# Two 16-head attention stages: the matrix products of a turn sorted by their kind, and the steps of all other chains moved to even turns, two turns apart

## The chip, the cores and the metric

The kernel runs on one core of a Trainium2 chip. The metric is the device time of one execution in microseconds (us), the median of several runs. Besides the runs there is one profiled execution of the kernel, whose trace holds every instruction of every engine: TensorE (PE, with its weight loads as PEld), VectorE (DVE), ScalarE (ACT), GpSimd (POOL), and SyncE (SP), which issues the DMAs.

## The reference

The reference is a chain of eight layers on an input of 16 sequences of 256 tokens with 128 features: four times an attention or mixing layer followed by a feed-forward layer. Each is wrapped as `x = x + layernorm(f(layernorm(x)))`. Two of the layers hold a causal softmax attention with 16 heads of 8 features, and only these are touched by the change. The first ("L2 attention") in full:

```python
q = (x @ Wq).reshape(b, t, h, d) * scale      # h = 16, d = 8, scale = d ** -0.25
k = (x @ Wk).reshape(b, t, h, d) * scale
v = (x @ Wv).reshape(b, t, h, d)
dot = einsum('bqhd,bkhd->bhqk', q, k)
dot = where(causal, dot, -inf)
out = einsum('bhqk,bkhd->bqhd', softmax(dot), v).reshape(b, t, h * d)
return out @ Wo
```

The second ("L3 attention") is the second half of a larger layer. Its keys and values have 4 heads, each used by 4 query heads; q and k go through an RMS norm over the 8 features of a head and a rotary embedding before the products, and the output is projected and added to its own input.

## The kernel before, in words

**Data.** The tokens lie in SBUF as `NG = 8` groups of 512 tokens; a group is two sequences, and a sequence with its 16 heads is a batch here. So each attention stage has 16 batches. Each stage is a function that issues instructions for one group or batch at a time, written as Python generators: a `yield` ends a step, and `idle(n)` yields n times, that is, it leaves n - 1 steps empty.

**The planner.** `turns` (L392) sets the order by hand. An item is a generator with a starting turn. In each turn every item that has started takes one step, or up to three if it is behind; the instructions are issued in exactly that order. The items of a stage (L429) are the batches, newest first, then the heads of the groups 1 to 7 (which prepare a group), and last a chain of unrelated work named `beside`. Batch b of group g starts at turn 12g + 6b; its head starts `early` turns before 12g, 10 in the first stage and 26 in the second, where it is behind at turn 0 and catches up three steps a turn.

**A batch** (`attention`, L435) in turns counted from its start:

- 0, 2, 4 ("by query"): for each of four sets of four heads, the product of 32 rows of qT with km (each head's keys, zeroed but for its own 8 features), 32x128 weights against 512 columns, into four PSUM banks; behind each of the four a product of a 128x128 mask with the identity adds the causal mask; then DVE takes the negative maximum of each bank (L459, `at_nm`).
- 5: POOL splits the maxima into three bf16 pieces (L467, L469). 8: a pair of 128x128 products brings these pieces (`at_pc`) into the other layout, and ACT writes them as `at_mT` (L476).
- 11, 13, 15 ("by key"): four products of 32 rows of kT with qm, to which four bf16 products of ones with `at_mT` add the negative maxima; then ACT takes the exponential of each bank (L491, `at_e`), and POOL sets the masked entries to zero (L497, a selection).
- 16 to 21 ("values"): products of 128x32 weights `at_vm` with `at_e` into the one bank `o`.
- 22: ACT copies `o` to `at_oT` (L521). 23: four transposes of it. 25: DVE takes the reciprocal of the sums and scales (L530, L532, `at_y`). 26: two transposes of `at_y`, and ACT's copy `at_yT`.
- After the second batch of a group, its `tail` projects `at_yT` with `wo`, and adds the result to x.

Six turns later the next batch does the same, so that in the steady state an even turn issues one batch's query products and an older one's values, and an odd turn one batch's key products and an older one's values. Every 12 turns one head and one tail are added.

**PSUM.** `RING_BANKS` gives seven banks to the tag "s", which the tags "mm" and "t" share, and one bank to "o". So the four query banks, the four key banks and every projection or transpose take a bank out of the same seven, and wait until the engine that read it last (DVE for the maxima, ACT for the exponentials and most copies) has released it.

**The heads.** In the first stage (`stage_l2_attn`): norm of x (DVE L255, L257 and POOL L244, L245, then DVE L264), transposes to `xT`, products with wk and wq, `km` and `qm` (`variants`, two ACT and one POOL instruction each), and the product with wv, whose result ACT spreads into `at_vm` (L390). Its `beside` first ends two groups of the stage before (two DMAs named back), and then builds a table `lm` for the next stage: for each of 16 heads ACT L1402, three turns later POOL L1405, two turns later DVE L1407. In the second stage the head is `l3_rotated`: RMS norm, transposes, four products with `qkv`, ACT's copies of them into one buffer (L1598), POOL's squares (L1604), DVE's sums (L1609), ACT's square root (L1612, with a load of its table ahead of it), DVE's scaling of qkv in place (L1616), POOL's products with the cosines (L1622, L1623), DVE's with the sines (L1625, L1626) and the sums (L1628, L1629); then transposes of `rot` give kT and qT.

All products are issued in `mm` (L336), so their rows are told apart by their tiles.

Of the kernel before, what the change touches and what calls it, by code (L numbers as in the profile page):

```python
# [185 lines left out]
def idle(n):  # L186

    for _ in range(n):
        yield
# [10 lines left out]
class Ctx:  # L200
# [191 lines left out]
    def turns(self, items):  # L392


        now = 0
        items = [[start, 0, steps] for start, steps in items]
        while items:
            for item in items[:]:
                for _ in range(min(3, now - item[0] + 1 - item[1])):
                    item[1] += 1  # L400
                    if next(item[2], self) is self:
                        items.remove(item)
                        break
            now += 1

    def attention_stage(self, head, early, first, tail, beside=iter(())):

        got = [{} for _ in range(NG)]
        heads = [head(g, got[g]) for g in range(NG)]
        for _ in range(first):
            next(heads[0])
        self.attention_pools()  # L420
        for _ in heads[0]:
            pass

        def batch(g, b):
            yield from self.attention(g, b, got[g])
            if b == 1:
                yield from tail(g, got[g]["yT"])

        items = [(12 * g + 6 * b, batch(g, b)) for g in range(NG) for b in range(2)]  # L429
        items = items[::-1] + [(12 * g - early, heads[g]) for g in range(1, NG)] + [(9, beside)]  # L430
        with self.tc.manual_schedule():
            self.turns(items)

    def attention(self, g, b, got):
# [14 lines left out]
        for i in range(3):  # L449

            t, q, keys, vs = (0, q0, q0, slice(0, 4)) if i == 0 else (1, q1, both, slice(2 * i - 2, 2 * i))
            ss = [self.ps("s") for _ in rows]
            for k, s in zip(rows, ss, strict=True):
                self.mm(s, qT[k, q], km[k, vs, keys], True, False)
            for r, s in enumerate(ss):
                n = vs.stop - vs.start
                s = s.rearrange("p (v n) -> p v n", v=n)
                self.mm(s[:, :, t * P :], ident, bc(negmask, 1, n), False, True)
                v_.tensor_reduce(nm[:, t, r, vs], s, AX.X, ALU.max, negate=True)  # L459
            if i < 2:  # L460
                yield from idle(2)
        yield
# [14 lines left out]
        yield from idle(3)  # L477
# [3 lines left out]
        for i in range(3):  # L481
# [19 lines left out]
            if i < 2:  # L501
                yield from idle(2)
        yield

        o = self.ps("o")
        for v in range(4):
            reg = SEQ * (v // 2)
            for r, k in enumerate(rows):
                e = es[v // 2][:, r].rearrange("p (v n) -> p v n", v=2)[:, v % 2, :]
                self.mm(o[k, reg : reg + SEQ], vm[:, 2 * b, v, k], e, v == 0, False)  # L510
            yield
        for v in range(4):
# [4 lines left out]
            if v % 2:  # L517
                yield
# [3 lines left out]
        yield  # L522
# [3 lines left out]
        yield from idle(2)  # L526
# [6 lines left out]
        yield  # L533
# [746 lines left out]
def stage_l2_attn(k, x, w, xs, decays):  # L1280
# [9 lines left out]
    def head(g, got):  # L1290
        yield
        if g == 0:
            xn = k.t([P, NT, D], "xn", 1)
            k.normed_act(xn, x[g], *k.kept)
            yield from idle(3)
        else:
            xn = yield from k.norm(x[g], "xn", 1, 2)
            yield
# [9 lines left out]
        yield  # L1308
# [4 lines left out]
        yield  # L1313
# [261 lines left out]
def l3_rotated(k, xa, w, bufs=1, pool=None):  # L1575


    nc, v = k.nc, k.nc.vector
    sq = k.t([P, NT, D], "rms_sq", min(bufs, 2))
    nc.gpsimd.tensor_tensor(sq, xa, xa, ALU.mult)  # L1580
    yield from idle(3)
# [7 lines left out]
    yield  # L1589
# [5 lines left out]
    for t in range(NT):  # L1595
# [3 lines left out]
        if t % 2:  # L1599
            yield  # L1600
# [10 lines left out]
    yield  # L1611
    nc.scalar.activation(ss, ss, AF.Sqrt)  # L1612
    yield
# [10 lines left out]
    yield  # L1624
    v.tensor_tensor(tmp[:, :, :, 0:4], x2, trig["sin"], ALU.mult)  # L1625
    v.tensor_tensor(tmp[:, :, :, 4:8], x1, trig["sin"], ALU.mult)  # L1626
    yield from idle(2)
# [5 lines left out]
def l3_gqa(k, x, xa, w, gain, mix, first):  # L1633
# [5 lines left out]
    def head(g, got):  # L1639
# [5 lines left out]
        yield  # L1645
# [3 lines left out]
        yield  # L1649
        got["qT"] = k.t([P, GT], "qT", 2)  # L1650
        v.tensor_scalar(got["qT"], k.transposed_ps(rot, slice(0, P)), gain, 1.0 / math.sqrt(8.0), ALU.mult, ALU.mult)  # L1651
        yield
# [29 lines left out]
    k.attention_stage(head, 26, 5, tail, next_mix(k, x[NG - 1], xa[NG - 1], mix, k.kept2))  # L1682
# [411 lines left out]
```

## Time and profile before

| what | value |
|---|---|
| median of 3 runs | 2936.19 us (2934.38 to 2936.97) |
| the profiled execution | 2931.63 us |
| its span, first to last instruction | 2929.9 us |
| mean granted TensorE clock | 0.968 |
| PE busy in the span | 2727.9 us, 23674 products |
| the two attention stages, turn by turn | about 1502 to 1833 us and 2304 to 2619 us of the span |

The page of the profile gives the busy time of each engine, and the costliest groups of instructions with "out<-in" by the program's tile names: `ps_s<-km,qT` is a query product, `ps_s<-qm,kT` a key product, `ps_s<-at_mT,b_rows` the addition of the maxima, `ps_s<-b_negmask,b_ident` a mask, `ps_o<-at_e,at_vm` a value product. The shape behind a product (32\*128, 128\*128, 128\*32) is rows by columns of its weights; an fp32 product is recorded as two passes, so that four of them show as x8. A line of the timeline is start, length, engine, line, operation, tiles, shapes and how many instructions were merged; in brackets the idle time before it and what ended it. A line of the windows is the stretch, its length, and for each engine its busy time with the number of instructions, then the granted TensorE clock, the DMA share and the GB/s. A product waiting for its bank can be counted as busy PE.

### The profile page before, as it was taken

The page shows a single profiled execution, that of the slowest core. Times are in us where ns is not written, and L with a number is a line of the kernel's source. Part 1 is how long each engine was busy: PE and PEld are TensorE (multiplying, and loading weights), DVE is VectorE, ACT ScalarE, POOL GpSimd, SP SyncE. Part 2 cuts the span into 40 slices and gives each one's busy share as a digit, 9 for nine tenths or more (in the row PEclk, how much of TensorE's full clock was granted, in tenths as well). Part 3 has the DMA queues.
Part 4 walks back from the last instruction along what each step waited for, and adds up shares of the span by engine and source line. Part 5 has one row for each costly group of instructions (what it writes and reads, how often), then busy time and mean ns, then how long its engine had stood idle before and what let it go on. Part 6 is the DMA issues. An engine that isn't in the chain of part 4 may idle for free.

```text
span 2929.9 us, 59646 instructions
## 1 busy us (share of the span) xinstructions
PE 2727.9 (93%) x23674; PEld 1842.9 (63%) x23674; DVE 1949.6 (67%) x5309; ACT 1713.0 (58%) x3568; POOL 1017.7 (35%) x1406
## 2 busy tenths in 40 slices
PE   8989999999998699999978997999999799989998
PEld 4556667766666588888843443566666444436897
DVE  5665666666676999999776674666574686737542
ACT  6756666666665577777635665444444377756443
POOL 3543333333345100000054554422231466645332
PEclk9999999999999799999989999899999899999999
DMA  3000000000000000000010000000000000010000
GB/s 105 12 1 2 1 1 2 2 2 2 5 12 27 6 14 11 10 11 9 20 61 5 1 1 1 1 1 1 1 1 1 2 1 1 1 36 23 1 16 16
DMA packets 30158, 31.30 MB, mean 11 GB/s; under 512 B 7404, under 2 KB 21292, under 8 KB 29868
## 3 DMA queue, kind: packets, MB, share of 16 engines
q1 hardware_dynamic: 29880, 27.49, 3.1%
q8 instruction: 187, 3.06, 0.4%
q14 instruction: 91, 0.75, 0.1%
HBM read 23.29 MB, written 4.19 MB: 9 GB/s over the span
## 4 chain that ended last, share of the span: by engine, by line
PE 71%; ACT 11%; DVE 11%; POOL 5%; issue 2%; DMA 0%; SPq 0%; POOLq 0%; ACTq 0%; DVEq 0%
PE ps_s L336 44%; PE ps_o L336 11%; PE ps_mm L336 7%; PE ps_s L325 3%; ACT e L949 2%; POOL ln_rs L245 1%; ACT at_e L491 1%; PE ps_t L1223 1%; DVE xn L264 1%; PE ps_xin L336 1%; POOL e L952 1%; PE ps_sum L336 1%; ACT L949 1%; ACT lg L1218 1%; DVE l_max L899 1%
## 5 line engine op out<-in xcount | busy, mean ns | idle before, releaser
L459 DVE TENSOR_REDUCE at_nm<-ps_s 128x2 f32<-128x512 f32 (+1 forms) x384 | 238.1, 681 | 119.7 <-PE ps_s L336 119.7
L491 ACT ACTIVATE at_e<-ps_s 128x512 f32<-128x512 f32 x384 | 198.1, 604 | 94.3 <-PE ps_s L336 92.1
L1507 DVE TENSOR_TENSOR scan<-ps_s,lm 128x384 f32<-128x384 f32 x256 | 124.6, 548 | 142.5 <-PE ps_s L336 142.2
L497 POOL TENSOR_SCALAR_AFFINE_SELECT at_e<-at_e 128x1024 f32<-128x1024 f32 (+1 forms) x96 | 135.1, 1407 | 208.6 <-ACT at_e L491 208.3
L245 POOL TENSOR_TENSOR ln_rs<-ln_rs,mhalf 128x4 f32<-128x4 f32 x192 | 196.0, 1021 | 15.8
L1031 POOL TENSOR_TENSOR ln_rs<-ln_mv,mendt 128x4 f32<-128x4 f32 x6 | 1.2, 198 | 510.6 <-DVE mend L1252 507.2
L244 POOL TENSOR_SCALAR ln_rs<-ln_mv 128x4 f32<-128x4 f32 x184 | 40.2, 219 | 372.7 <-DVE ln_mv L257 354.3
L899 DVE TENSOR_REDUCE l_max<-ps_s 128x3 f32<-128x384 f32 x256 | 124.7, 550 | 51.5 <-PE ps_s L336 49.1
L336 PE MATMUL ps_o<-my,meT 128*128 128x129 f32 x1024 | 142.2, 284 | 15.3 <-ACT mgot L1237 7.9
L952 POOL TENSOR_SCALAR_AFFINE_SELECT e<-e 128x512 f32<-128x512 f32 x128 | 78.9, 637 | 217.2 <-ACT e L949 217.2
L336 PE MATMUL ps_s<-km,qT 32*128 32x512 f32 x768 | 139.5, 677 | 11.8 <-DVE qT L1651 3.7
L336 PE MATMUL ps_s<-qm,kT 32*128 32x512 f32 x768 | 142.5, 644 | 8.0 <-DVE at_nm L459 7.8
L336 PEld LDWEIGHTS ps_o<-my,meT 128*128 128x128 f32 x1024 | 125.8, 192 | 38.1 <-ACT meT L1225 24.4
L336 PE MATMUL ps_mm<-mdisp,mxn 128*128 128x128 f32 x1024 | 129.6, 284 | 10.5 <-DVE mdisp L1139 10.4
L336 PEld LDWEIGHTS ps_o<-l_w,mlp_h 128*128 128x128 f32 x1024 | 125.9, 192 | 19.1 <-issue 12.8
L336 PE MATMUL ps_o<-at_e,at_vm 128*32 128x128 f32 (+1 forms) x2048 | 122.9, 337 | 15.3 <-ACT at_oT L521 15.3
L336 PE MATMUL ps_s<-mphi,mxT 128*128 128x256 f32 x448 | 123.2, 395 | 14.2 <-DVE mpart L1100 13.9
L336 PE MATMUL ps_o<-l_w,mlp_h 128*128 128x128 f32 x1024 | 130.1, 276 | 4.0 <-ACT oT L969 3.9
L336 PEld LDWEIGHTS ps_mm<-mdisp,mxn 128*128 128x128 f32 x1024 | 124.6, 200 | 14.0 <-DVE mdisp L1139 11.9
L336 PE MATMUL ps_s<-b_negmask,b_ident 128*128 128x256 bf16 (+1 forms) x640 | 124.9, 305 | 8.1 <-DVE b_negmask L780 1.4
L1484 ACT COPY BT<-ps_s 128x512 f32<-128x512 f32 x64 | 37.5, 587 | 158.1 <-PE ps_s L336 158.1
L336 PEld LDWEIGHTS <-b_ident 128*128 128x128 bf16 x656 | 57.2, 99 | 109.2 <-issue 91.3
(471 smaller groups left out, 7266.5 us busy)
## 6 DMA issues: line engine op xcount, KB each, us to landing
mw<-in_l1fw SPq DMA_DIRECT2D x16, 256.0 KB, 2.6
moe_w<-in_moe SPq DMA_DIRECT2D x16, 256.0 KB, 5.3
l_w<-in_l SPq DMA_DIRECT2D x10, 256.0 KB, 3.4
x<-in_x SPq DMA_DIRECT2D x8, 256.0 KB, 4.3
xs<-x SPq DMA_DIRECT2D x8, 256.0 KB, 2.3
out<-x SPq DMA_DIRECT2D x8, 256.0 KB, 2.3
slT<-xs SPq DMA_DIRECT2D x6, 256.0 KB, 2.6
mphi<-in_l1f SPq DMA_DIRECT2D x7, 128.0 KB, 2.0
```

Source lines behind the costliest of these rows:

```text
L244: g.tensor_scalar(out, in_, scale, eps, ALU.mult, ALU.add)
L245: g.tensor_tensor(out, out, self.mhalf[:, :n], ALU.pow)
L325: self.nc.tensor.transpose(out[:n, k * P : (k + 1) * P], src[:, k, cols], self.c["ident"])
L336: self.nc.tensor.matmul(out, lhsT=lhsT, rhs=rhs, start=start, stop=stop, skip_group_check=True)
L459: v_.tensor_reduce(nm[:, t, r, vs], s, AX.X, ALU.max, negate=True)
L491: nc.scalar.activation(e[:, r], s, AF.Exp)
L497: nc.gpsimd.affine_select(at, at, [[0, 4], [0, n], [1, P]], ALU.is_ge, 0.0, base=0, channel_multiplier=-1)
L899: v.tensor_reduce(mx[:, b, :, h, 16], s, AX.X, ALU.max, negate=True)
L949: nc.scalar.activation(e[:, h].rearrange("p j n -> p (j n)"), s[:, : 3 * P], AF.Exp)
L952: nc.gpsimd.affine_select(e[:, :, j, :], e[:, :, j, :], [[0, 4], [1, P]], ALU.is_ge, 0.0, base=0, channel_multiplier=-1)
L1484: nc.scalar.copy(s, ps)
L1507: v.tensor_tensor(m, s[:, : SEQ + P], lm[:, SCAN_HEADS[4 * (t // 2) + 2 * i + hh], :], ALU.mult)
```

## The change

`turns` takes a list of kinds for even and one for odd turns. A generator's `yield` may name the kind of its next step; in a turn all items are sorted by the kind of the step that comes next (a stable sort: within a kind the order is as before), steps without a name having the kind `None`. An item may also carry a turn ahead of which it doesn't step at all. The order is loose steps, query products, values, key products in even turns, and values, key products, loose steps, query products in odd turns.

In `attention` the mask products are issued ahead of the four query products and start the sum in their banks; a turn's kinds are named in the yields; the transposes of `at_oT` come two turns after the copy (turn 24 instead of 23), with the reciprocal and the scaling in the same turn (24 instead of 25). The turns of the products by query (0, 2, 4), by key (11, 13, 15) and of the values (16 to 21) are those of before.

The heads have their steps in even turns: in the first stage the norm and wq come a turn earlier; in the second, most waits in `l3_rotated` become longer, so that the head starts 30 turns ahead instead of 26, and the head of group g takes no step before turn 4g - 4. The products with the cosines and sines stand in one odd turn, and in the next turn stand the first qkv copies of the group behind. `apart` keeps the old waits where `l3_rotated` is called by another stage. `beside` starts at turn 10 instead of 9.

```diff
-    def turns(self, items):
+    def turns(self, items, kinds=None):
         now = 0
-        items = [[start, 0, steps] for start, steps in items]
+        items = [[item[0], 0, *item[1:], *(None, 0)[len(item) - 2 :]] for item in items]
         while items:
-            for item in items[:]:
+            order = [item for item in items if item[4] <= now]
+            if kinds:
+                order.sort(key=lambda item: kinds[now % 2].index(item[3]))
+            for item in order:
                 for _ in range(min(3, now - item[0] + 1 - item[1])):
                     item[1] += 1
-                    if next(item[2], self) is self:
+                    item[3] = next(item[2], self)
+                    if item[3] is self:
...
-        items = [(12 * g + 6 * b, batch(g, b)) for g in range(NG) for b in range(2)]
-        items = items[::-1] + [(12 * g - early, heads[g]) for g in range(1, NG)] + [(9, beside)]
+        items = [(12 * g + 6 * b, batch(g, b), "by query") for g in range(NG) for b in range(2)]
+        items = items[::-1] + [(12 * g - early, heads[g], None, 4 * g - 4) for g in range(1, NG)] + [(10, beside)]
         with self.tc.manual_schedule():
-            self.turns(items)
+            self.turns(items, ([None, "by query", "values", "by key"], ["values", "by key", None, "by query"]))
...
+            for s in by_variant:
+                self.mm(s[:, :, t * P :], ident, bc(negmask, 1, n), True, False)
             for k, s in zip(rows, ss, strict=True):
-                self.mm(s, qT[k, q], km[k, vs, keys], True, False)
-            for r, s in enumerate(ss):
-                n = vs.stop - vs.start
-                s = s.rearrange("p (v n) -> p v n", v=n)
-                self.mm(s[:, :, t * P :], ident, bc(negmask, 1, n), False, True)
+                self.mm(s, qT[k, q], km[k, vs, keys], False, True)
+            for r, s in enumerate(by_variant):
                 v_.tensor_reduce(nm[:, t, r, vs], s, AX.X, ALU.max, negate=True)
...
         nc.scalar.copy(oT, o)
-        yield
+        yield from idle(2)
         tp = self.ps("mm")
         for j in range(4):
             nc.tensor.transpose(tp[:, j * P : (j + 1) * P], oT[:, j * P : (j + 1) * P], self.c["ident"])
-        yield from idle(2)
...
+    apart = lambda n, even: idle(n if pool else even)
     sq = k.t([P, NT, D], "rms_sq", min(bufs, 2))
     nc.gpsimd.tensor_tensor(sq, xa, xa, ALU.mult)
-    yield from idle(3)
+    yield from apart(3, 4)
...
-    yield
+    yield from apart(1, 0)
     v.tensor_tensor(tmp[:, :, :, 0:4], x2, trig["sin"], ALU.mult)
     v.tensor_tensor(tmp[:, :, :, 4:8], x1, trig["sin"], ALU.mult)
-    yield from idle(2)
+    yield from apart(2, 3)
...
-    k.attention_stage(head, 26, 5, tail, next_mix(k, x[NG - 1], xa[NG - 1], mix, k.kept2))
+    k.attention_stage(head, 30, 6, tail, next_mix(k, x[NG - 1], xa[NG - 1], mix, k.kept2))
```

## The prediction, made before the change was run

> **What bounds the kernel now.** I read the page first: TensorE is busy for 93% of the span and no other engine comes near. The change touches two stages only, so I then asked for the busy times of two long windows (the two 16-head attentions), and of one regular stretch of 12 turns in each (key products to key products, two batches).
>
> ```profile
> PE 2727.9 (93%) x23674; PEld 1842.9 (63%) x23674; DVE 1949.6 (67%) x5309; ACT 1713.0 (58%) x3568; POOL 1017.7 (35%) x1406
> 1502.00:1833.00 331.00, 298.39 (x2503) 131.71 (x2504) 215.59 (x526) 187.56 (x405) 171.57 (x243) 0.93 0.04 11
> 2304.00:2619.00 315.00, 291.71 (x2490) 132.79 (x2493) 205.22 (x324) 207.94 (x463) 182.33 (x216) 0.97 0.00 1
> 1673.03:1708.23 35.20, 34.83 (x314) 15.57 (x313) 25.12 (x58) 22.75 (x51) 19.72 (x27) 1.00 0.00 1
> 2471.22:2507.27 36.05, 35.62 (x320) 16.22 (x317) 26.30 (x42) 26.40 (x59) 22.69 (x26) 1.00 0.01 2
> ```
>
> The stages are 646 of 2930 us. In the regular stretches TensorE shows as full, but a product counts as busy while it waits for its bank, so I read the single products in the timeline:
>
> ```profile
> 1605.87 1.14 PE L336 MATMUL ps_s<-qm,kT 32*128 32x512 f32 x8
> 1606.83 0.39 PE L336 MATMUL ps_s<-at_mT,b_rows 32*128 32x512 bf16 x4
> 1607.15 0.65 PE L336 MATMUL ps_o<-at_e,at_vm 128*32 128x128 f32 x16
> 1607.73 1.13 PE L336 MATMUL ps_s<-xT,l_wq 128*128 128x512 f32 x2
> 1608.79 1.14 PE L336 MATMUL ps_s<-km,qT 32*128 32x512 f32 x8
> 1609.86 0.61 PE L336 MATMUL ps_s<-b_negmask,b_ident 128*128 128x256 bf16 x4
> 1610.40 0.64 PE L336 MATMUL ps_o<-at_e,at_vm 128*32 128x256 f32 x8
> 1610.97 1.16 PE L336 MATMUL ps_s<-l_wo,at_yT 128*128 128x128 f32 x8
> ```
>
> Start to start: key block 1.28, values 0.58, wq 1.06, query rows 1.07, masks 0.54, values 0.57. Three shapes alternate: 32 rows, 128x128, 32 columns. In the single records, 512-column bf16 products of one shape follow each other at 0.215; to the next shape it takes 0.309. The same 0.09 to 0.10 stands at every change of shape, and the first weights after it load in the open: 0.10 before fp32 rows or a 512-column fp32 product, 0.06 before transposes, 0.03 before values, 0.01 before a mask. Adding blocks without waits, the 12 turns need 31.8 us in the first stage and 32.1 in the second; the remaining 3.4 and 3.9 are waits for PSUM banks, which ACT and DVE empty:
>
> ```profile
> 1607.30 2.06 ACT L491 ACTIVATE at_e<-ps_s 128x512 f32<-128x512 f32 x4 [0.74 <-PE ps_s L336]
> 1609.23 0.62 ACT L521 COPY at_oT<-ps_o 128x512 f32<-128x512 f32 x1
> 1609.50 2.16 DVE L1407 TENSOR_SCALAR lm<-lm,dt 128x384 f32<-128x384 f32 x1
> 1611.59 2.47 DVE L459 TENSOR_REDUCE at_nm<-ps_s 128x2 f32<-128x512 f32 x4
> 1609.44 2.01 POOL L497 TENSOR_SCALAR_AFFINE_SELECT at_e<-at_e 128x2048 f32<-128x2048 f32 x1 [3.66 <-ACT at_e L491]
> ```
>
> The exponentials begin 1.43 after the first key product, 0.49 apart, 0.60 long. The lm row takes 2.16 where POOL's selection runs beside it, 0.39 elsewhere.
>
> **What the change saves.** Per 12 turns: (a) six pairs of value blocks come to lie side by side (end of an even turn, start of the odd one): 6 x (0.095 + 0.027) = 0.73. (b) The loose 128x128 blocks (projections, transposes) now stand ahead of the masks, the same shape. First stage seven blocks (at_oT twice, at_y, at_y with wk, wq, wo, wv with xn): 7 x 0.095 + 4 x 0.06 + 3 x 0.10 = 1.20; second stage nine (three of them 0.10 loads): 1.5. (c) Back: where a loose block is now first after the drain, it loads in the open in place of a mask: 0.2 and 0.3. Sum 1.7 and 1.9. Masks before the query rows instead of behind cost nothing by themselves: same products, as many changes. No arithmetic, no DMA and no SP work moves; the two back DMAs go one turn later. Extra empty turns (the longer idles, the start 30 instead of 26 turns ahead) issue nothing. Over 96 turns less the ramps, 6.5 such lots: -24 us if nothing else waits longer.
>
> **What it costs: banks.** The Trainium skill, TensorEngine Tiling (Array Packing), section Tiling Modes, says that a change of tiling mode drains TensorE; alone that gives the -24. The same page, Performance Considerations (PSUM Bottleneck), speaks against it: tiling speeds up the products, not the emptying of PSUM. The rows side with the second: four exponentials need 2.06 and four maxima 2.47 for blocks of 1.28 and 1.61. Before, values and loose blocks lie between keys and queries, and the exponentials run beside them. Now only loose blocks do; both value blocks lie between queries and keys.
>
> I wrote out 12 turns. There are seven banks. When queries begin, keys hold four, three are free, loose tiles take from those, and the last mask needs a bank of exponential number f (f loose tiles still held). Exponential r frees its bank at 1.43 + 0.49r + 0.60 + 0.06 (signal) = 2.09, 2.58, 3.07, 3.56 after the keys' start; then the mask and the drain, 0.21 (0.32 with 512 columns). Keys to queries, first stage, by turn:
> - 4, no loose block: 2.09 + 0.21 = 2.30 (products alone 1.84)
> - 0, at_oT, wide masks: 2.58 + 0.32 = 2.90
> - 2, pc and at_y, both read by ACT behind the exponentials: 3.07 + 0.21 = 3.28 (products 2.17)
> - 10, wo: products, 2.81
> - 8, pc, at_y, wk, wq: the last bank is wq's, which ends at 3.53; latency 0.25, qT 0.69: 4.74
> - 6, at_oT, wv, xn, wide masks: products 4.09, plus 1.6: DVE's lm step now stands ahead of the maxima in turn 4, POOL's selection ends near 5.5, so the first maximum ends near 6.6 where keys start at 5.1.
> Sum 21.7. Queries to keys: 6 x 2.09 = 12.5, plus values waiting for the at_oT copy behind the exponentials (3.39 + 0.62 + 0.06 = 4.07, against 3.37): 0.7 and 0.2. Total 35.1, against 35.20 now.
>
> Second stage: turn 2 with one more transpose 3.77; turn 4 (half of qkv) 3.28; turn 8 3.9; turn 10 2.8; turn 0 4.4, because km, two table loads (1.28 each in the trace, for Sqrt and back to Exp) and exponentials queue on ACT; turn 6 5.4, because the qkv copies of the next group (turn 4) now come one turn behind the cosine products that read the old qkv (two before): POOL's selection until 5.4, then 1.05 + 1.50, holds ACT and so the next exponentials. 23.6 + 12.6 = 36.2, against 36.05. So the bank waits take back what the drains give. The trace of before can't show which bank the planner picks; its waits fit the pick of the bank that is free first, which I take. In fixed order turn 8 would wait for pc's four mT copies (3.39 + 1.57, +0.2), and in the second stage keys for the qkv copies at 8.4 instead of starting at 5.3 (with turn 8, +3.5); those are the upper bounds. If waits do not grow, -1.7 and -1.9 are the lower. Behind a waiting mask stand the query rows and values, and for them DVE; behind a qkv copy on ACT stand the exponentials.
>
> The reciprocal and products of y move into the turn of their transposes, 0.9 on DVE ahead of the maxima; those start only after masks and rows (1.6), so I take 0, and 0.9 per six turns if that cover is gone. Stats, norms, wq and qT move by a turn with two turns to spare: 0, at worst one turn, 2.1.
>
> **What it costs: the opening of the second stage.** There heads catch up three steps a turn, and loose blocks now stand ahead of the queries, so each query block waits for a head's whole chain. Now: qkv scaled at 2338.8, maxima, sine and sums until 2343.6, first keys 2347.98. After: the scaling ends near 2337; then in one line n 0.9, its transposes and masks 1.4, query rows 1.4, maxima 2.5, sine and sums 2.8, rotated transposes 1.0, the other half of qkv 1.0, masks 0.5 = 2348.5; a pair of query blocks 2.1 + 1.1: keys at 2351.7, +3.7. The next three pairs carry group 3's qkv behind cosines, 0.8 each: +6 in all. Bounds: -2 (another chain ends last) to +10. The first stage's heads start two turns into it and don't catch up: 0.
>
> **Clock.** A long wait can cost half speed:
>
> ```profile
> 1638.60:1642.00 3.40, 3.40 (x21) 1.14 (x14) 0.44 (x1) 1.73 (x4) 1.61 (x3) 0.50 0.00 0
> ```
>
> It follows the one regular key block that waited 1.8 us. The new order has such waits of 1.6 every 12 turns; I put two windows at 1.7: +3; bounds 0 and +15.
>
> **Sum.** 6.5 x (-0.1) + 6.5 x 0.15 + 6 + 3 = +9. The profiled execution took 2931.63 (span 2929.9); with +9, 2941. The median, 2936.19, lies 4.6 above it; the prediction is on the median: 2945.
>
> **Rivals.** (1) Faster: the waits stay as they are and the drains are gained. It decides where exponential r frees its bank before the masks get there: if they began 0.5 us earlier, or masks found banks free, the turns with no or two loose tiles would lose nothing. For it: the drains are certain. Against: 2.06 for four exponentials is in every turn. Whole: 2936 - 24 + 3 = 2915; half of it: 2928. 15%. (2) The banks go out in fixed order, so that pc and qkv tiles, read late, block: +0.2 and +3.5 per 12 turns, 6.5 x 3.7 + 6 + 3 = +33: 2969. For it: the picks are planned ahead without the true times; against: today's waits. 17%. (3) The balance is struck and the opening hides beside DVE's chain: 2936 +- 6. 23%. Forecast, 2942 to 2955: 45%.
> Within 0.2% (5.9 us, about what a measurement of this kernel can tell from no change): 25%, with the forecast's lower edge. Faster 15%, slower 60%. The range 2930 to 2968 leaves out 13% below and 7% above.
>
> **What would show it.** Right: value blocks side by side with no 0.09 between; masks spread over more than 0.33 in turns 2 and 4; key blocks with a wait after the lm step; regular stretches within 1 us of 35.2 and 36.05; first keys of the second stage later by 3 to 6. Wrong: stretches at 33.5 and 34.2 (rival 1), or the second at 39 (rival 2).

## The result, and the profile after

The changed kernel takes 2944.21 us (median of 6 runs, 2941.59 to 2947.13) beside 2934.59 us for the kernel before (6 runs, 2931.99 to 2936.97). The ratio is 1.0037, with a 95% interval of 1.0027 to 1.0047: 9.6 us slower, which is little but more than 0.2%. The profiled execution took 2944.25 us, 12.6 more than that of before.

The first row is from the page of the changed kernel. The others are from its windows (stretch, length, busy PE, PEld, DVE, ACT and POOL with their instructions, granted clock, DMA share, GB/s): the first attention, the second, and a regular stretch of 12 turns of each, key products to key products.

```profile
PE 2691.4 (91%) x23674; PEld 1831.2 (62%) x23674; DVE 1928.5 (66%) x5309; ACT 1704.6 (58%) x3566; POOL 1013.3 (34%) x1406
```

```profile
1502.00:1833.00 331.00, 281.22 (x2556) 129.64 (x2556) 202.22 (x546) 188.06 (x411) 173.19 (x247) 0.93 0.04 11
2304.00:2640.00 336.00, 280.80 (x2504) 127.45 (x2500) 196.31 (x322) 198.13 (x449) 172.51 (x209) 0.92 0.00 1
1661.54:1695.31 33.77, 31.28 (x320) 14.18 (x316) 22.25 (x58) 22.31 (x50) 19.67 (x28) 1.00 0.00 1
2467.61:2505.08 37.47, 33.10 (x324) 15.39 (x320) 26.16 (x42) 25.97 (x60) 22.25 (x27) 1.00 0.01 1
```

Busy TensorE went down by 36.5 us (2727.9 to 2691.4) while the time went up: by this view TensorE stands idle for longer (a product that waits for its bank can count as busy, so this alone doesn't say where the time went). The 12 turns tell where: 35.20 became 33.77 in the first stage, and 36.05 became 37.47 in the second. Measured in the trace from the first query product to the end of the last output projection, the first stage went from 310.0 to 296.2 (13.8 less; the masks, which now stand ahead of the first query product, take 1.0 of it back) and the second from 310.4 to 336.6 (26.1 more). The rest of the profiled difference lies outside: some 2.5 us stand by 212 us of the span already, where nothing is changed (they stand there in e1 and e2 below as well, but not in e11). The parts between and behind the stages are 1.1 and 1.9 us shorter.

So one stage won and the other lost. The theory to test was this. A: the first stage won because the drains at changes of shape went; the second lost through the opening, through the qkv copies one turn behind the cosines, and through the table loads beside km. The rivals were that only one of the two edits (sorting, new places of the heads' steps) does harm, and that the masks or the table `lm` bring the gain.

### The profile page after: what moved, and what is told of

It reads as the page before. It is cut to its first block, busy times and chain, and to the rows that moved or that the text cites. A ratio compares the mean times of both kernels' runs of the same rounds, so it can differ in the third digit from the quotient of the medians.

```text
span 2942.4 us, 59570 instructions
## 1 busy us (share of the span) xinstructions
PE 2691.4 (91%) x23674; PEld 1831.2 (62%) x23674; DVE 1928.5 (66%) x5309; ACT 1704.6 (58%) x3566; POOL 1013.3 (34%) x1406
## 4 chain that ended last, share of the span: by engine, by line
PE 68%; ACT 14%; DVE 11%; POOL 5%; issue 2%; DMA 0%; POOLq 0%; ACTq 0%; DVEq 0%
PE ps_s L336 42%; PE ps_o L336 11%; PE ps_mm L336 7%; ACT at_e L503 4%; PE ps_s L325 3%; ACT e L961 2%; POOL ln_rs L245 2%; DVE xn L264 1%; PE ps_t L1235 1%; PE ps_xin L336 1%; POOL e L964 1%; PE ps_sum L336 1%; ACT L961 1%; DVE ln_st L255 1%; DVE l_max L911 1%
## 5 line engine op out<-in xcount | busy, mean ns | idle before, releaser
L336 PE MATMUL ps_s<-b_negmask,b_ident 128*128 128x256 bf16 (+1 forms) x640 | 142.0, 305 | 41.8 <-ACT at_e L503 23.6
L336 PEld LDWEIGHTS ps_o<-my,meT 128*128 128x128 f32 x1024 | 125.8, 192 | 38.1 <-ACT meT L1237 24.4
L336 PE MATMUL ps_s<-qm,kT 32*128 32x512 f32 x768 | 131.7, 660 | 17.8 <-DVE at_nm L470 11.8
L1495 ACT COPY BT<-ps_s 128x512 f32<-128x512 f32 x64 | 37.5, 587 | 158.1 <-PE ps_s L336 158.1
L336 PE MATMUL ps_s<-xT,l_w 128*128 128x512 f32 x256 | 124.3, 606 | 1.3 <-ACT xT L823 1.3
L264 DVE TENSOR_SCALAR xn<-z,ln_mv,ln_rs 128x128 f32<-128x128 f32 x252 | 74.9, 360 | 70.1 <-POOL ln_rs L245 70.1
L336 PE MATMUL ps_o<-at_e,at_vm 128*32 128x128 f32 (+1 forms) x2048 | 105.1, 335 | 15.6 <-ACT at_oT L534 11.4
```

Of the source, the lines that this page charges most:

```text
L264: self.nc.vector.tensor_scalar(out[:, k, :], src[:, k, :], mv[:, k, 0:1], rs[:, k : k + 1], ALU.subtract, ALU.mult)
L336: self.nc.tensor.matmul(out, lhsT=lhsT, rhs=rhs, start=start, stop=stop, skip_group_check=True)
```

## The experiments

"Before" is the median of the kernel before on the same chip beside it; the lengths are from each kernel's one profiled execution, as above. "Opening" is first query to first key product in the second stage, and the last column is the fifth regular stretch of 12 turns there, with a head in it.

| kernel | us | before | first stage | its 12 turns | second stage | opening | its 12 turns |
|---|---|---|---|---|---|---|---|
| before | 2934.6 | | 310.0 | 35.2 | 310.4 | 32.8 | 36.0 |
| changed | 2944.2 | 2934.6 | 296.2 | 33.8 | 336.6 | 39.8 | 37.5 |
| e1 first stage only | 2916.4 | 2935.8 | 296.2 | 33.8 | 310.9 | 32.8 | 36.1 |
| e2 second stage only | 2956.7 | 2935.8 | 309.7 | 35.2 | 339.4 | 39.8 | 39.1 |
| e3 second sorted only | 2931.2 | 2935.8 | 298.2 | 33.8 | 328.9 | 39.8 | 37.5 |
| e4 second spaced only | 2945.2 | 2935.8 | 296.2 | 33.8 | 338.3 | 42.4 | 40.1 |
| e5 first unsorted | 2922.7 | 2931.7 | 297.7 | 34.2 | 312.8 | 34.7 | 36.1 |
| e6 cosines earlier | 2932.4 | 2931.7 | 296.3 | 33.8 | 324.3 | 41.4 | 36.8 |
| e7 no square root | 2945.4 | 2931.7 | 296.2 | 33.8 | 337.8 | 41.0 | 39.7 |
| e8 sorted from turn 12 | 2926.6 | 2931.7 | 296.3 | 33.8 | 318.2 | 32.3 | 37.0 |
| e9 before, table later | 2927.7 | 2933.0 | 303.2 | 34.9 | 310.7 | 32.8 | 36.1 |
| e10 masks behind | 2933.8 | 2933.0 | 311.9 | 35.7 | 310.2 | 34.7 | 36.1 |
| e11 second body only | 2917.4 | 2933.0 | 296.3 | 33.8 | 309.4 | 32.2 | 36.1 |
| e12 three mended | 3092.2 | 2934.0 | 296.2 | 33.8 | 473.2 | 61.2 | 58.5 |

The totals repeat only to several us: the part ahead of the first stage, the same in all, ends between 1512.4 and 1519.4. So small differences are read from the stages. Where the code is the same, the first stage repeats to 0.3 (but for e3, 2.0 longer), the second only to some 3: the old one took 310.2 to 312.8 in five traces, the changed one 336.6 here and 339.4 in e2. The second differs where TensorE's granted clock was half. These are the fourth and the fifth stretch of e2, where the changed kernel, with the same code, took 37.47 each at a clock of 1.00:

```profile
2476.80:2517.54 40.74, 36.37 (x320) 16.71 (x316) 26.21 (x42) 25.99 (x60) 22.61 (x27) 0.92 0.01 2
2517.54:2556.60 39.06, 34.62 (x321) 15.69 (x317) 24.59 (x41) 26.00 (x60) 21.30 (x26) 0.96 0.00 1
```

So differences of the second stage under some 3 us are not read as a gain or a loss. The one profiled execution of e3 lay 9.8 above that kernel's own median, and its second stage began 5.4 later than in e1.

**e1, the change in the first stage alone.** The second stage uses the old `attention`, heads and item list.

```diff
-    k.attention_stage(head, 30, 6, tail, next_mix(...))
+    k.attention_stage_old(head, 26, 5, tail, next_mix(...))
```

> The first attention as in the changed kernel, the second exactly as before. Theory A (the two stages moved in opposite directions: the first won about 13 us because the drains went and the bank waits hardly grew, the second lost about 26): 2922, between 2918 and 2926, with the 12 turns of the first stage at 33.8. Rival (the prediction's balance of about -1 in the first stage; what the trace shows more is one half-clock window less and an offset): 2930 to 2935.

Measured: 2916.4 against 2935.8, ratio 0.9942 (0.992 to 0.9964), 1.6 below the expected range. From the windows of e1, a regular stretch of each stage:

```profile
1661.21:1694.98 33.77, 31.27 (x316) 14.17 (x312) 22.24 (x59) 22.34 (x50) 19.70 (x28) 1.00 0.00 1
2477.83:2513.88 36.05, 35.62 (x318) 16.22 (x317) 26.32 (x42) 26.42 (x58) 22.74 (x27) 1.00 0.00 1
```

The first stretch is the changed kernel's, the second the old one's, and half of the change is an improvement.

**e2, the second stage alone.**

```diff
-    k.attention_stage(head, 10, 4, tail, beside())
+    k.attention_stage_old(head, 10, 4, tail, beside())
```

> The second attention as in the changed kernel, the first exactly as before. Theory A: 2934.6 + 24 to 27 = 2958 to 2962. Rival (each stage near the prediction's terms, +9 to +10 from the second stage): 2944. If the loss of the second stage comes from what the first leaves behind, it vanishes here: 2935.

Measured: 2956.65, ratio 1.0074 (1.0059 to 1.0089), 21 above before. The second stage is 29 longer by itself; the loss is not left over from the first. By the totals the two halves add up to +1.5 and not to the +9.6 of both together; the intervals of e1 and e2, some 6 and 4 us to either side, are wide enough for that, and by the stages they add up to +15 beside +12.

**e3 and e4, sorting and spacing apart in the second stage.** The body of `attention` is new in both. e3 also takes back the new waits in the heads (not printed here) and their hold (`hold=100` holds no head).

```diff
 e3
...
-    k.attention_stage(head, 30, 6, tail, next_mix(...))
+    k.attention_stage(head, 26, 5, tail, next_mix(...), at=9, hold=100)
 e4
...
-            self.turns(items, (...))
+            self.turns(items, kinds if sort else None)
...
-    k.attention_stage(head, 30, 6, tail, next_mix(...))
+    k.attention_stage(head, 30, 6, tail, next_mix(...), sort=False)
```

> The first stage new; in the second stage the sorting by kinds and the masks first, but the heads' steps, their start and the start of the table as before. Theory A (the opening is lost to loose blocks sorted ahead of the queries; the regular stretches to the new places of the heads' steps, qkv copies one turn behind the cosines): opening still about +15, stretches back to 34 to 35: 2922 + 15 - 8 = 2929, between 2924 and 2936. Rival (the sorting itself is what the stretches lose by, through the banks): 2944 or more. Rival (the places of the steps are all of the loss): 2915 or less.

> The first stage new; in the second stage the heads' new steps and starts and the masks first, but no sorting: in each turn batches first, newest first, then the heads. Theory A: the opening is back near 33 to 35 from first query to first keys, the wait for the qkv copies stays (about 2.5 every 12 turns while there are heads, 5 lots), drains as before: 2922 + 12 = 2934, between 2928 and 2942. Rival (the sorting is all of the loss): 2922. Rival (the places of the steps are all of it): 2945 or more.

Measured: e3 2931.17, ratio 0.9994 (0.9985 to 1.0002); e4 2945.2, ratio 1.003 (1.0018 to 1.0041). Each edit alone lengthens the stage (328.9 and 338.3, against 309.4 with neither, e11), the new places of the heads' steps by more; and with those, sorting costs nothing further (336.6 and 339.4). (By the totals e3 is 14.8 above e1, by the stages 18.0.) Theory A's division (opening to the sorting, stretches to the spacing) is wrong: the opening is longer with either alone. The timelines of TensorE in the opening tell how, first before (idle time and what ended it in brackets), then the changed kernel:

```profile
2324.60 1.05 PE L325 MATMUL ps_s<-const_ident,n 128*128 128x128 f32 x4 [2.88 <-DVE n L1588]
2332.46 0.60 PE L325 MATMUL ps_s<-const_ident,n 128*128 128x128 f32 x4
```

```profile
2310.89 1.11 PE L325 MATMUL ps_s<-const_ident,n 128*128 128x128 f32 x4 [5.24 <-DVE n L1601]
2326.86 1.08 PE L325 MATMUL ps_s<-const_ident,n 128*128 128x128 f32 x4 [7.35 <-DVE n L1601]
2327.74 1.91 PE L336 MATMUL ps_s<-b_negmask,b_ident 128*128 128x512 bf16 x4
2336.21 1.07 PE L325 MATMUL ps_s<-const_ident,rot 128*128 128x128 f32 x8 [3.79 <-DVE rot L1642]
```

Before, the norms of groups 1 and 2 are worked out side by side, and the second is ready when TensorE comes to it. In the changed kernel the wait of 5.24 is for the first group's norm, which is not late (its transposes start 7.3 us behind the first query product, 9.4 before); the second query block, which filled this time before, is now sorted behind it. The wait of 7.35 is for the second group's. Its head takes no step before turn 4, so its norm starts when the first one's qkv is done, and TensorE, whose next query products stand behind these transposes, waits for it with nothing else to do. e4 has much the same waits without any sorting (no run took the hold away without the other new waits), and then e3, where no head is held but each query block waits for the loose blocks sorted ahead of it:

```profile
2311.57 1.09 PE L325 MATMUL ps_s<-const_ident,n 128*128 128x128 f32 x4 [4.48 <-DVE n L1602]
2328.67 1.09 PE L325 MATMUL ps_s<-const_ident,n 128*128 128x128 f32 x4 [7.52 <-DVE n L1602]
```

```profile
2316.83 1.12 PE L325 MATMUL ps_s<-const_ident,n 128*128 128x128 f32 x4 [8.23 <-DVE n L1599]
2327.89 1.09 PE L325 MATMUL ps_s<-const_ident,n 128*128 128x128 f32 x4 [3.10 <-DVE n L1599]
2340.20 1.18 PE L336 MATMUL ps_s<-l_qkv,nT 128*128 128x288 f32 x2 [3.70 <-ACT qkv L1609]
```

**e5, the first stage without its sorting.** The second stage is the old one, here and in e10.

```diff
-            self.turns(items, ([None, "by query", "values", "by key"], ["values", "by key", None, "by query"]))
+            self.turns(items)
```

> The second stage as before; the first stage with everything of the change (masks first, the transposes two turns later, the heads' steps in even turns) but the sorting: in a turn batches newest first, then heads. Theory A (the first stage's 13.6 are the drains that the sorting saves): the regular 12 turns are back near 35.2 and the time is 2916.4 + 13 = 2929, between 2925 and 2935. Rival (the masks first, or the heads' even turns, bring it): 12 turns near 33.8, time within 4 of 2916.

Measured: 2922.73 against 2931.71, ratio 0.9969 (0.9956 to 0.9981). Windows of e5:

```profile
1661.56:1695.76 34.20, 33.23 (x319) 14.61 (x316) 24.57 (x58) 22.75 (x50) 19.89 (x28) 1.00 0.00 1
```

34.20 is nearer to the sorted 33.77 than to 35.20. Theory A falls for the first stage: with the rest of the change in place the sorting is worth only 0.43 per 12 turns, and what stands beside it 1.0. The whole stage wins 1.5 by the sorting: the 12 turns behind the first keys are 3.0 longer with it (45.3 against 42.3).

**e9, the kernel before with the table one turn later.**

```diff
-        items = ... + [(9, beside)]
+        items = ... + [(at, beside)]
-    k.attention_stage(head, 10, 4, tail, beside())
+    k.attention_stage(head, 10, 4, tail, beside(), 10)
```

> The kernel before with one number changed: beside starts at turn 10 instead of 9 in the first attention, so that its lm step on VectorE meets POOL's selection at another point. Theory B (most of the 1.0 by which the unsorted first stage beat the old one per 12 turns is this step, 2.16 beside a selection and 0.4 elsewhere): lm at 0.4 nearly everywhere, 12 turns at 34.2 to 34.6, the first stage near 304, the time 4 to 7 below the kernel before. Rival (the masks first or the heads' even turns bring the 1.0): 12 turns at 35.2, no change beyond 2.

Measured: 2927.66 against 2933.04, ratio 0.9982 (0.9972 to 0.9992); 12 turns 34.88. The DVE timeline of e9, and then that of the changed kernel, over one regular stretch:

```profile
1662.28 2.68 DVE L264 TENSOR_SCALAR xn<-x,ln_mv,ln_rs 128x128 f32<-128x128 f32 x4 [0.92 <-POOL ln_rs L245]
1679.51 0.95 DVE L1407 TENSOR_SCALAR lm<-lm,dt 128x384 f32<-128x384 f32 x1
1695.84 0.41 DVE L1407 TENSOR_SCALAR lm<-lm,dt 128x384 f32<-128x384 f32 x1
```

```profile
1676.40 0.41 DVE L1418 TENSOR_SCALAR lm<-lm,dt 128x384 f32<-128x384 f32 x1
1692.24 1.40 DVE L264 TENSOR_SCALAR xn<-x,ln_mv,ln_rs 128x128 f32<-128x128 f32 x4 [0.30 <-POOL ln_rs L245]
1693.57 0.41 DVE L1418 TENSOR_SCALAR lm<-lm,dt 128x384 f32<-128x384 f32 x1
```

One number brings 5.4 us, but only 0.3 of the stretch's 1.0, a third: lm takes 0.95 and 0.41 instead of 2.16 and 0.39, and xn is as long as before. The stage is 6.8 shorter, more than seven stretches of 0.3: the 12 turns behind the first keys and those with the half clock shown in the prediction fell too (45.2 to 41.9, and 38.1 to 36.2). In the changed kernel both steps that stretched beside POOL have come out short: lm 0.41, and the four products of xn 1.40 instead of 2.68.

**e10, the masks behind the query rows again, still sorted.**

```diff
-            for s in by_variant: self.mm(s[:, :, t * P :], ident, bc(negmask, 1, n), True, False)
             for k, s in zip(rows, ss, strict=True):
-                self.mm(s, qT[k, q], km[k, vs, keys], False, True)
+                self.mm(s, qT[k, q], km[k, vs, keys], True, False)
+            for s in by_variant: self.mm(s[:, :, t * P :], ident, bc(negmask, 1, n), False, True)
```

> The kernel with the first attention new and the second as before, but the masks of the first behind the query rows again, still sorted. Theory B (the place of the masks is worth one change of shape in each even turn, 6 x 0.1 per 12 turns, and no more): 12 turns 34.4 instead of 33.77, first stage 300, time 4 above the 2916.4 of that kernel beside the same kernel before (ratio about 0.995 to 0.996). Rival (the masks first take bank waits away, the prediction's zero being wrong): 12 turns 35 or more, first stage 305 or more.

Measured: 2933.78 against 2933.04, ratio 1.0001 (0.9991 to 1.0011); 12 turns 35.65, stage 311.9. The rival is right: the place of the masks is worth 1.88 per 12 turns, and without it the sorted order is no better than the old one. The lm and xn steps are as short in e10 as in the changed kernel (lm 0.41 but once), so that in this order short steps alone win nothing. TensorE's timeline in turn 8, first the changed kernel, then e10:

```profile
1671.09 0.49 PE L336 MATMUL ps_s<-b_negmask,b_ident 128*128 128x256 bf16 x3
1672.64 0.27 PE L336 MATMUL ps_s<-b_negmask,b_ident 128*128 128x256 bf16 x1 [1.06 <-ACT at_mT L487]
1672.84 1.14 PE L336 MATMUL ps_s<-km,qT 32*128 32x512 f32 x8
1673.91 1.08 PE L336 MATMUL ps_o<-at_e,at_vm 128*32 128x128 f32 x32
```

```profile
1681.34 1.23 PE L336 MATMUL ps_s<-km,qT 32*128 32x512 f32 x6
1682.90 1.12 PE L336 MATMUL ps_s<-km,qT 32*128 32x512 f32 x2 [0.33 <-ACT at_mT L624]
1683.96 0.61 PE L336 MATMUL ps_s<-b_negmask,b_ident 128*128 128x256 bf16 x4
1684.50 1.08 PE L336 MATMUL ps_o<-at_e,at_vm 128*32 128x128 f32 x32
```

Both wait for one late bank, the pieces' tile that ACT reads. A query row alone (x2) takes as long as four side by side: 1682.90 to 1683.96 is 1.06, and 1672.84 to 1673.91 is 1.07. So a late bank costs a row 1.06 with 0.54 of masks behind it, 1.60 until the values; a mask waiting for the same bank is through in 0.20 and the four rows go together, 1.27. The difference, 0.33, is what this turn differs by (7.28 against 7.61 from one key block to the next). From one key block to the next, from turn 0 on, the six intervals of the stretch differ by 0.64, 0.33, 0, 0.43, 0.33 and 0.14.

**e6, the cosines two turns earlier.**

```diff
-    yield from idle(2)
+    yield from apart(2, 0)
     v.tensor_tensor(qk, qk, bc(ss.rearrange("p (t h) -> p t h", t=NT), 3, 8), ALU.mult)
...
-    yield from apart(2, 3)
+    yield from apart(2, 5)
```

> The changed kernel with the scaling of qkv in the turn of its reciprocal, and so cosines and sines two turns earlier, three turns ahead of the next group's qkv copies instead of one. Theory A (ACT waits 2.5 us every 12 turns for the cosines to release the one qkv buffer, and that delays the key products): the key block of turn 5 loses its wait of 2.7; five stretches with heads, so 2944.2 - 10 to -13 = 2931 to 2934. Rival (another wait is right behind it, so nothing is won): 2942 to 2946. Rival (two heads' work crowds VectorE one turn earlier): above 2946.

Measured: 2932.41 against 2931.71, ratio 0.9998 (0.9989 to 1.0007), 9 less than the changed kernel's excess. In the changed kernel TensorE's timeline has, in turns 4 to 6 of a regular stretch,

```profile
2485.57 1.55 PE L336 MATMUL ps_s<-qm,kT 32*128 32x512 f32 x6
2488.31 0.69 PE L336 MATMUL ps_s<-qm,kT 32*128 32x512 f32 x1 [1.20 <-ACT qkv L1611]
...
2488.85 0.59 PE L336 MATMUL ps_s<-qm,kT 32*128 32x512 f32 x1
```

and ScalarE's and POOL's timelines of the same turns have

```profile
2487.86 0.70 ACT L1611 COPY qkv<-ps_s 128x288 f32<-128x288 f32 x2 [2.51 <-POOL rot L1636]
2489.48 2.06 ACT L503 ACTIVATE at_e<-ps_s 128x512 f32<-128x512 f32 x4 [0.92 <-PE ps_s L336]
```

```profile
2483.80 2.01 POOL L509 TENSOR_SCALAR_AFFINE_SELECT at_e<-at_e 128x2048 f32<-128x2048 f32 x1 [4.73 <-ACT at_e L503]
2485.78 1.05 POOL L1635 TENSOR_TENSOR rot<-qkv,const_cos 128x512 f32<-128x512 f32 x1
2486.78 1.05 POOL L1636 TENSOR_TENSOR rot<-qkv,const_cos 128x512 f32<-128x512 f32 x1
```

Read from the bottom: the selection until 2485.81, the cosines until 2487.83, the qkv copies, and then the last key product, which waits for a bank that a qkv tile holds. The four maxima of the turn before had given back all their banks by 2487.13 (2484.65 and 2.48 long), so the bank was not picked for being free first. In e6 ScalarE's and TensorE's timelines have

```profile
2515.50 0.73 ACT L1611 COPY qkv<-ps_s 128x288 f32<-128x288 f32 x2
```

```profile
2515.83 1.27 PE L336 MATMUL ps_s<-qm,kT 32*128 32x512 f32 x7
2516.81 0.59 PE L336 MATMUL ps_s<-qm,kT 32*128 32x512 f32 x1
```

The copies no longer wait, the last key product starts 0.98 behind the first instead of 3.28, and turn 6 takes 4.14 from keys to queries instead of 6.44. The second stage is 12.3 shorter, far more than the 3 by which the same code differs: this cause is shown. In the stretch from which these lines come only 0.7 of turn 6's 2.3 is left (36.76 for 37.47), since e6 runs at half clock in a part of turn 0, as the changed kernel does not:

```profile
2500.00:2504.00 4.00, 3.51 (x26) 1.00 (x25) 3.17 (x5) 1.91 (x4) 1.79 (x5) 0.69 0.00 0
```

A second buffer for qkv wasn't tried.

**e7, no square root, and so no table loads.**

```diff
-    nc.scalar.activation(ss, ss, AF.Sqrt)
+    nc.scalar.activation(ss, ss, AF.Copy)
```

> The changed kernel with a copy in place of the square root, so that the norm's scaling is another and the output with it; ScalarE then loads no table for it and none back for the exponentials. Theory A (turn 0 of the stretches with heads is 4.75 from keys to queries, against 2.9 without, because two table loads of 1.28 stand ahead of the exponentials): -1.9 in each of about 6 stretches: 2944.2 - 11 = 2933, between 2930 and 2937. Rival (the loads lie beside other waits): 2942 to 2946.

Measured: 2945.37 against 2931.71, ratio 1.0042 (1.003 to 1.0055): nothing won. ScalarE's timeline in turn 0, the changed kernel and then e7:

```profile
2468.25 1.28 ACT L1625 ACT_TABLE_LOAD   x1
2469.54 0.31 ACT L1625 ACTIVATE ss<-ss 128x128 f32<-128x128 f32 x1
2469.87 1.28 ACT L503 ACT_TABLE_LOAD   x1
2471.16 2.07 ACT L503 ACTIVATE at_e<-ps_s 128x512 f32<-128x512 f32 x4
```

```profile
2470.41 0.34 ACT L1625 ACTIVATE ss<-ss 128x128 f32<-128x128 f32 x1
2471.28 2.06 ACT L503 ACTIVATE at_e<-ps_s 128x512 f32<-128x512 f32 x4 [0.52 <-PE ps_s L336]
```

Turn 0 does become 1.94 shorter (4.76 to 2.82), as expected. It is given back in the same stretch: turn 2 goes from 3.75 to 4.61 and turn 6 from 6.44 to 8.08, where the cosines are as late as ever and the wait is now followed by products at half speed. Windows over 3.4 us behind that wait, the changed kernel and then e7:

```profile
2489.75:2493.15 3.40, 3.40 (x24) 1.68 (x27) 2.84 (x5) 3.40 (x8) 1.53 (x2) 1.00 0.03 7
```

```profile
2491.00:2494.40 3.40, 3.40 (x12) 2.29 (x12) 2.28 (x4) 3.40 (x8) 1.53 (x2) 0.55 0.01 2
```

In the sixth stretch, where both kernels have the full clock, the gain stands whole (31.25 for 33.19). So the loads do cost what was expected; elsewhere the wait of turn 2 and the clock take it back (69 us of the stage at half clock, 54 in the changed kernel).

**e8, sorting only from turn 12, old places of the heads' steps.** The heads' old waits are not printed here.

```diff
-            if kinds:
+            if kinds and now >= opening:
...
-    k.attention_stage(head, 30, 6, tail, next_mix(...))
+    k.attention_stage(head, 26, 5, tail, next_mix(...), at=9, hold=100, opening=12)
```

> The first stage new; in the second the heads' steps, starts and waits as before, and the sorting only from turn 12 on. Theory A (sorting the opening costs 7 from first query to first keys and several more behind it): the opening is 32.8 again, and against the kernel that sorts from turn 0 (2931.2) it wins 7 to 10: 2921 to 2924. Against the kernel that changes the first stage alone (2916.4) it shows what the sorting is worth in the regular stretches of the second stage: theory A, near 0 to +6; rival (the drains are gained there as in the first stage): 2910 or less.

Measured: 2926.63 against 2931.71, ratio 0.998 (0.9971 to 0.9989). The opening is 32.3, so sorting the opening does cost 7.5 with the old spacing. But the stage is 318.2, 8.8 longer than without sorting (e11). The 12 turns behind the first keys are 5.0 longer (37.1 against 32.1), the sixth stretch 2.2 and the last five key blocks 3.0; the four stretches between differ by 0.9 at the most, and the rest is shorter. TensorE had half the clock for 42 us of the stage, and for 23 in e11.

**e11, the new body of a batch alone in the second stage.** As e3, without kinds.

> The first stage new; in the second only the body of the batches new (masks first, transposes of at_oT a turn later), neither sorted nor with the heads' new steps. Theory (both the sorting and the spacing lose in the second stage, the body alone is worth about nothing there): the second stage 309 to 312, like the kernel that changes the first stage alone, ratio 0.993 to 0.996. Rival (the body alone wins as it did in the unsorted first stage): second stage 302 to 306, ratio 0.990 to 0.992. Rival (the opening suffers from the masks first): second stage above 315.

Measured: 2917.35 against 2933.04, ratio 0.9941 (0.9926 to 0.9956); stage 309.4. The body alone does no harm; 309.4 lies too near to the 310.2 to 312.8 of the old one to be a gain. This and e1 are the two fastest versions, and can't be told apart (e5, e8 and e9 are faster than the kernel before as well, by less).

**e12, three causes mended together.** As e6; no sorting and no holding of heads before turn 12; and POOL's power in place of the square root:

```diff
-    v.tensor_scalar(ss, ss, 1.0 / 8, RMS_EPS, ALU.mult, ALU.add)
...
-    nc.scalar.activation(ss, ss, AF.Sqrt)
...
-    v.reciprocal(ss, ss)
+    k.rsqrt(ss, ss, 1.0 / 8, RMS_EPS)
```

> The changed kernel with its three suspected losses in the second stage taken away together: the cosines two turns earlier, POOL's power of -0.5 in place of VectorE's scaling, ScalarE's square root and VectorE's reciprocal (no table load), and in the first 12 turns of the second stage no sorting and no holding of a head. Theory A (the second stage loses by these three, and taking one away alone only moves a wait to the next): opening 32 to 34, stretches with heads 33.5 to 35, keys of turn 0 to 2 at 2.9 from keys to queries, the second stage 303 to 310, the time 2914 to 2922 beside 2933 before, ratio 0.993 to 0.996. Rival (sorting loses in the second stage whatever is mended, since ScalarE and POOL carry more there): stretches 36 or more, second stage 318 or more. Open: POOL's power of 128 elements, of which the trace has only 4 elements at 1.0 us; if it takes over 4 us, the selections behind it wait and the rival's numbers come for another reason.

Measured: 3092.16 against 2933.95, ratio 1.0538 (1.0521 to 1.0556). POOL's timeline shows why:

```profile
2498.77 20.78 POOL L245 TENSOR_TENSOR ss<-ss,mhalf 128x128 f32<-128x128 f32 x1
2521.65 1.10 POOL L509 TENSOR_SCALAR_AFFINE_SELECT at_e<-at_e 128x1024 f32<-128x1024 f32 x1
```

The power of 128 elements a partition took 20.78 us, and the selections stood behind it. The run tells nothing of whether the three causes add up; that stays open.

## Why the prediction was right in its total and wrong in both stages

The forecast was 2945.0, within 0.8 of the median, with slower at 60%. The total is right by luck, because two wrong terms balance: the first stage was put at 6.5 x (-0.1), about -1, and measured -13.8; the second at 6.5 x 0.15 + 6, about +7, and a part of the +3 for the clock, and measured +26.1. Of the prediction's own signs of being right, the values side by side and the masks spread over turns 2 and 4 are in the trace. The wait behind the lm step is not, both stretches are 1.4 off where 1 was allowed, and the first keys of the second stage came 6.9 later, not 3 to 6. The first stage stands near the sign of the first rival (33.5).

- **Drains.** The values do lie side by side: the trace merges both blocks of a pair into one row (x32 above). That bank waits take back what the drains give fits the sorting with the masks behind: 35.65 against 35.20 (e10, with the other moves of the first stage in it).
- **Turn 6, "plus 1.6: DVE's lm step".** This is the step that failed in the first stage's sum: turn 6 measured 4.07, not 5.7, since lm takes 0.41 and ends as POOL's selection begins. This one term is more than the whole difference between the 35.1 forecast and the 33.77 measured. The other turns of the first stage came out as worked out (2.88, 3.26, 2.28, 2.81 for 2.90, 3.28, 2.30, 2.81), but for turn 8. The keys and the queries of turn 6 in the changed kernel:

```profile
1661.50 1.14 PE L336 MATMUL ps_s<-qm,kT 32*128 32x512 f32 x8
1665.57 1.14 PE L336 MATMUL ps_s<-km,qT 32*128 32x512 f32 x8
```

- **"Masks before the query rows instead of behind cost nothing by themselves."** This failed too. The count of products and shapes was argued, not what a late bank costs the product that waits for it. In the sorted order it is worth 1.88 per 12 turns (e10), more than the whole gain of 1.43. It did not enter the 35.1, though, whose turns were worked out with the masks ahead.
- **The pick of the bank.** "The bank that is free first, which I take" failed twice, and the fixed order that the prediction kept as a bound was right in kind. Turn 8 waits for the pieces' tile: 5.20, not 4.74. (The bound of +0.2 for it was itself too small: its 3.39 + 1.57 leave out the signal, the mask and the drain, 0.06 + 0.21, with which they make 5.23.) The key block of turn 5 waits for the qkv copies: turn 6 of the second stage 6.44, not 5.4. The other turns there were right or near (3.75, 3.26, 3.86, 2.81; turn 0 4.76 for 4.4). The stretch is 37.47 for 36.2; the +3.5 of the second rival was too large.
- **The opening.** +6 was forecast, in one chain of a head; measured are 7 to the first keys and 10.2 in the next 12 turns (43.9 for 33.7), then 2.9 and 2.2. The chain is in the trace as it was written out, the second group's norm right behind the first one's scaling. From the end of the scaling to the first keys it takes 17.3 us where 14.7 were forecast; four masks in it took 1.91 (shown above), and 1.03 at full clock. Two things were wrong. Sorting is not the only cause: e4, without it, opens even later. And the next 12 turns were put at 2.4 (e2, with the same code, needs 6.9 more than before, and e6 4.3).
- **Clock.** +3 stood for two windows at 1.7. By the clock records of the traces TensorE had half the clock for 54.2 us of the second stage, before for 20.3. It comes in windows of 3.4 us or a multiple of it, so these are ten more. (In the first stage there were two fewer, one of them in the stretch of 38.1.) The price was right: the two windows in e2's fourth stretch cost it 3.3 and the one in the fifth 1.6. Ten at 1.6 are an estimate of 16 of the 26.1, and an upper one, since some fall into waits. By this estimate the number of windows is the term of the second stage that was mis-sized most. What brings a window, and what does not, stays open.
- **The end of the second stage**, with no heads left, was taken as unchanged. The last two stretches took 33.2 and 30.6, against 33.6 and 32.2, but the five key blocks behind them 21.6 against 17.0, with 10.2 us at half clock against none.

What is not settled is how much of the first stage's gain in e5 is the masks, the shorter xn or the lm step where nothing is sorted (lm alone gave a third), how much of the second stage's loss is the half clock and whether its causes add up, and why in its stretches with heads sorting loses with the old spacing.

## What to carry to other kernels

Where several engines share a ring of banks, put the product that is through soonest first into each bank, so that a late bank holds up little work: that was worth more here (1.88 per 12 turns) than sorting for fewer changes of shape (0.43). A chain that catches up, three dependent steps a turn, belongs beside other work (or ahead of the stage, which was not tried), and a step moved to a tidy place can land one turn behind the reader of a buffer that it overwrites: look at each buffer with a single copy before moving its writer. A total that comes out right proves none of its terms; change one stage or one edit at a time, as e1 did, to find that half of a change is worth keeping. Read the granted clock of a stretch before its length: the same code took 37.47 or 40.74.

## What was not expected of the hardware

- A query row of 32x512 in fp32 took 1.06 us alone and 1.07 with three others beside it.
- POOL's power took 1.0 us for 4 elements a partition and 20.78 for 128, about 0.16 us an element (19.8 / 124).
- The same wait of 2.7 us on TensorE was followed by full speed in the changed kernel and by a granted clock of 0.55 in e7, where another wait of 1.05 stood two key blocks ahead; the length of one wait doesn't tell.
- Taking two table loads of 1.28 out of every stretch shortened the turn that they were in by 1.94, a stretch at full clock in both kernels by as much (33.19 to 31.25), and the whole by nothing.
